# Half-width broadcasts doubled by ScalarE, and a reordered start and end, in a window-attention and mixture-of-experts kernel

## The chip, the cores and the metric

The kernel runs on 1 core of one Trainium2 chip. The metric is the device time of one execution in microseconds. Three runs of the kernel before gave 4324.14, 4325.08 and 4339.78: a median of 4325.08 us.

## What is computed

The input `x` is 2 images of 128 channels and 256 x 256 pixels in fp32. Two residual blocks follow each other:

```python
x = x + _L0_conv_ref(_ln_c(x), W_qkv, W_out, rel_height, rel_width)
t = tokens(x)                       # one token of 128 channels per pixel
t = t + _L0_ffn_ref(_ln_t(t), router_w, router_b, expert_w, expert_b)
```

`_ln_c` and `_ln_t` subtract the mean over the 128 channels and divide by the standard deviation. The first block is attention of 8 x 8 windows over 12 x 12 key windows, with 4 heads of 32 channels and relative position logits, masked so that each query pixel sees only keys of every second row and column. The second one routes each token: a softmax over 8 experts, the best two kept and scaled to sum to 1, and the sum of the two experts' 128 x 128 products weighted so.

## The kernel before

**Tiling.** Channels lie on the 128 partitions. The pixels are cut into 64 strips of 8 image rows (32 for each image), and each strip into 4 planes, the pixels of equal parity in rows and columns; the mask makes planes independent in the attention. A step of the main loop (L811) does the attention of plane `n` (256 in all) and a share of everything else, so that each engine has work at all times. Two image rows (512 tokens) are called a row here and written (strip, k), k from 0 to 3. The loop runs 7 steps past the last plane for what is left of the last rows.

**What a step holds.** For plane n: the scores (`scores`, L464, matmuls of L476 and L493), their exponential `pT` (L501), the weighted sums (`attend`, L505, matmuls of L514 and L524) and, on VectorE, the chain of sum transposed (L534), reciprocal, transposed back (L539) and output `o` (L544); then the output projection `po` (L552), added into `xt` (L557). For plane n+1: values, position products, keys and queries (`project`, L399: `pv` L349, `pu` L408, `pk` L422, `pq` L447), with ScalarE copying values, keys (`kcol`, L433 and L443) and queries (`qs`, L449) out of PSUM. The values go to DRAM (`send_values`, L368) and come back as key windows `vwin` (`take_values`, L380). For one finished row and one row that the attention will need: squares on ScalarE (L576), sums by matmul (`norms`, L565, L582), and their inverse deviations on VectorE and ScalarE (`rstd`, L222).

**The experts' way through the steps.** In the step after its norms a row is routed (`route`, L608: logits, their exponential on ScalarE at L620, ranks, gates), and gates, mean and rates are transposed and written to DRAM (`spread`, L650). They are read back as broadcasts, the same 512 numbers on every partition: the rates `rb` of the first norm (`fetch_rstd`, L664), the mean `sb` (`fetch_means`, L693) and the eight gates `gb` (`fetch`, L682). In each `fetch` an engine writes one column of the buffer first, so that the DMA's wait for the buffer is taken by that engine. A step later `means` adds the mean to the row (L701), `times` multiplies by each gate (L707, six on VectorE, experts 5 and 7 on GpSimd), and eight matmuls sum up in one bank of PSUM (`product`, L716), experts 0 to 3 at the end of that step, 4, 6, 7 and 5 in the next one. `end` (L722) adds them to the row, and `store` (L752) writes it out. GpSimd also applies the first norm (`ln1`, L273) to rows of coming strips.

**What sets the order.** Inside the main loop the order of every engine's instructions is the order of the program (`tc.manual_schedule`, L810). The helpers are generators, and the loop advances them piece by piece with `next`. Ahead of the loop a scheduler orders the instructions. Nearly all DMAs are issued from SP's queue, in order: one that waits for a landing holds up those behind it. L825 aligns TensorE's instruction stream at the start of each step from step 6 to the last plane: it fills up with NOPs until the next instruction has slot 157 in a block of 256.

**Start.** Ahead of the loop stand the loads of `x` and of the weights, the preparation of the weights (L157 to L196), the first norms of the rows of strip 0 and of two more (`first_norms`, L282, three stages each: squares, sums and a copy; statistics; spreading by transposes and `ln1`), and the projection of plane 0.

Of the kernel before, what the change touches and what calls it, by code (L numbers as in the profile page):

```python
# [17 lines left out]
P = 128  # L18
HEADS, DH = 4, 32
E = 8  # L20
# [26 lines left out]
BLOCK, FIRST_LIMIT = 256, 99  # L47
NU = 9


@with_exitstack
def kernel(
# [46 lines left out]
    nc.scalar.preload_act_table_set("natural_log_exp_and_others")  # L99

# [37 lines left out]
    for j in range(4):  # L138
# [17 lines left out]

    wmean = ctile([P, 3, 1], "wmean")  # L157
    nc.vector.tensor_reduce(wmean, wall[:, 0:3, :], AX.X, ALU.add)
    nc.vector.tensor_scalar_mul(wmean, wmean, 1.0 / C)
    nc.vector.tensor_tensor(  # L160
        wall[:, 0:3, :], wall[:, 0:3, :], wmean.broadcast_to([P, 3, P]), ALU.subtract
    )
    wt = ctile([P, 4, P], "wt")
    pw = mm_tile("pw")
    for j in range(4):
        nc.tensor.transpose(pw[:, j * P : (j + 1) * P], wall[:, j, :], ident)
    nc.vector.tensor_copy(wt.rearrange("p j c -> p (j c)"), pw)
    nc.vector.tensor_scalar_mul(wt[:, 0, :], wt[:, 0, :], SCALE)
    wq, wk, wv, wo = (wt[:, j, :] for j in range(4))

    relT = []
    for rname, rsb in zip(("relh", "relw"), relsb):
        pr = mm_tile(f"p_{rname}")
        nc.tensor.transpose(
            pr[:, :n_rel], rsb.rearrange("r h d -> r (h d)"), ident[:n_rel, :n_rel]
        )
        rT = ctile([P, n_rel], f"{rname}T")
        nc.vector.tensor_scalar_mul(rT, pr[:, :n_rel], SCALE)  # L180
        relT.append(rT)
    mid = n_rel // 2
    lo = mid - 2 * (PR - 1)
    relbd = ctile([P, P], "relbd")
    nc.gpsimd.memset(relbd, 0.0)
    for h in range(HEADS):
        hp = slice(h * DH, (h + 1) * DH)
        for j in range(2):
            c0 = h * DH + NU * j
            nc.vector.tensor_copy(  # L190
                relbd[hp, c0 : c0 + NU], relT[j][hp, lo : lo + 2 * NU - 1 : 2]
            )
    wrel = ctile([P, P], "wrel")
    pr = mm_tile("p_wrel")
    nc.tensor.matmul(pr[:, :P], lhsT=wall[:, 0, :], rhs=relbd, start=True, stop=True)
    nc.vector.tensor_copy(wrel, pr[:, :P])  # L196
# [368 lines left out]
    def norms(f, c, nm):  # L565
# [13 lines left out]
        plt = mm_tile(f"plt{nm}")  # L579
# [84 lines left out]
    def fetch_rstd(gd, nm):  # L664

        rb = gates.tile([P, NT * P], F32, tag="rb", name=f"rb{nm}", bufs=2)
        nc.sync.dma_start(rb, to_all(gd, E + 1))
        return rb

    def to_all(gd, j):  # L670

        return gd[j * NT : (j + 1) * NT].rearrange("r k -> (r k)").partition_broadcast(P)

    class Experts:
# [7 lines left out]
        def fetch(self, e, eng):  # L682
# [8 lines left out]
            nc.sync.dma_start(self.gb[e], to_all(self.gd, e))  # L691

        def fetch_means(self):  # L693

            self.sb = gates.tile([P, NT * P], F32, tag="sb", name="sb%d_%d" % self.at, bufs=1)
            nc.sync.dma_start(self.sb, to_all(self.gd, E))  # L696
# [28 lines left out]
    class NoExperts:  # L725
        def fetch(self, e, eng):
            pass

        def fetch_means(self):
            pass  # L730
# [15 lines left out]

    to_store = []
# [9 lines left out]


# [14 lines left out]
    for _ in range(3):  # L773
# [36 lines left out]
    with tc.manual_schedule(engines={ET.PE, ET.DVE, ET.Activation, ET.Pool, ET.SP}):  # L810
        for n in range(n_planes + 7):  # L811
# [12 lines left out]
            if 6 <= n < n_planes:  # L824
# [5 lines left out]
            if gated and gated[0]:  # L830
                rout = route(*gated[0], *gated[2])
            next(rout, None)
            nxt.fetch(5, nc.scalar)
            for _ in rout:
# [3 lines left out]
            nxt.fetch(7, nc.scalar)  # L838
            if gated:
# [10 lines left out]
            next(ahead, None)  # L850
            next(ahead, None)
            for e in (4, 6, 7, 5):
                ex.product(e)


            f = (i - 1, pl) if 0 < i <= len(strips) else None
            c = row_at(n)
            if f or c:
                norm = norms(f, c, f"_{n}")
# [104 lines left out]
```

## Time and profile before

| | |
|---|---|
| median of three runs | 4325.08 us |
| the profiled execution | 4331.68 us |
| its span, first to last instruction | 4329.9 us |
| TensorE busy, 94,273 matmuls | 4220.6 us (97%) |
| VectorE busy | 3790.8 us (88%) |
| ScalarE busy | 1320.4 us (30%) |
| GpSimd busy | 1087.9 us (25%) |
| granted TensorE clock, mean | 0.991 |
| DMA: moved | 1022.17 MB, mean 236 GB/s |
| gates `gb`: 2,048 loads of 256 KB, issue to landing | 5.7 us (median) |
| means `sb`: 256 loads of 256 KB | 4.5 us |
| rates `rb`: 249 loads of 256 KB | 3.5 us |

An instruction's row tells its start, its length, its engine and line, what it writes and reads, and in brackets how long the engine stood idle before it and what ended that. PE is TensorE, PEld its weight loads, DVE VectorE, ACT ScalarE, POOL GpSimd, SP the queue that issues DMAs. "issue" means that the engine waited for nothing that the profile shows.

### The profile page before, as it was taken

The page shows a single profiled execution, that of the slowest core. Times are in us where ns is not written, and L with a number is a line of the kernel's source. Part 1 is how long each engine was busy: PE and PEld are TensorE (multiplying, and loading weights), DVE is VectorE, ACT ScalarE, POOL GpSimd, SP SyncE. Part 2 cuts the span into 40 slices and gives each one's busy share as a digit, 9 for nine tenths or more (in the row PEclk, how much of TensorE's full clock was granted, in tenths as well). Part 3 has the DMA queues.
Part 4 walks back from the last instruction along what each step waited for, and adds up shares of the span by engine and source line. Part 5 has one row for each costly group of instructions (what it writes and reads, how often), then busy time and mean ns, then how long its engine had stood idle before and what let it go on. Part 6 is the DMA issues. An engine that isn't in the chain of part 4 may idle for free. (4 is left out here: it accounts for less than half of the span.)

```text
span 4329.9 us, 224393 instructions
## 1 busy us (share of the span) xinstructions
PE 4220.6 (97%) x94273; PEld 2464.3 (57%) x94273; DVE 3790.8 (88%) x11850; ACT 1320.4 (30%) x3774; POOL 1087.9 (25%) x1126
## 2 busy tenths in 40 slices
PE   7899999999999999999999999999999999999987
PEld 5455555555555555555555555555555555555553
DVE  5798898898888889988889889898888898888877
ACT  3223333332333333233332333333323232333321
POOL 1222222222222222222222222222222222222211
PEclk9999999999999999999999999999999999999999
DMA  4787878788787877878788787887878788787865
GB/s 112 212 245 241 248 236 246 241 244 248 235 239 240 247 236 248 248 235 251 240 247 241 243 247 238 247 248 239 247 233 246 233 250 244 239 246 239 245 190 190
DMA packets 824578, 1022.17 MB, mean 236 GB/s; under 512 B 137634, under 2 KB 409634, under 8 KB 823594
## 3 DMA queue, kind: packets, MB, share of 16 engines
q1 hardware_dynamic: 822864, 1007.52, 76.5%
q8 instruction: 769, 12.60, 1.3%
q14 instruction: 215, 1.76, 0.1%
q10 hardware_dynamic: 730, 0.29, 0.0%
HBM read 863.78 MB, written 143.75 MB: 233 GB/s over the span
## 5 line engine op out<-in xcount | busy, mean ns | idle before, releaser
L716 PE MATMUL acc<-xe,ew 128*128 128x512 f32 x4096 | 1918.4, 601 | 20.7 <-DVE gb L690 14.5
L716 PEld LDWEIGHTS acc<-xe,ew 128*128 128x128 f32 x4096 | 758.4, 190 | 940.3 <-issue 872.7
L707 DVE TENSOR_TENSOR xe<-xs,gb 128x512 f32<-128x512 f32 x1536 | 950.4, 685 | 11.2 <-PE acc L716 1.6
L711 POOL COPY last<-xe 128x1 f32<-128x1 f32 x256 | 47.6, 186 | 3120.0 <-DVE gb L690 3110.9
L707 POOL TENSOR_TENSOR xe<-xs,gb 128x512 f32<-128x512 f32 x512 | 652.1, 1275 | 1.5 <-PE att L524 1.0
L493 PE MATMUL att<-qs,kcol 32*60 32x32 f32 x32768 | 395.3, 223 | 16.7 <-issue 15.9
L493 PEld LDWEIGHTS att<-qs,kcol 32*60 32x60 f32 x32768 | 390.3, 127 | 21.1 <-issue 20.5
L275 POOL TENSOR_TENSOR xn<-xt,rb 128x512 f32<-128x512 f32 x249 | 374.0, 1502 | 93.5 <-DMA rb<-gd 92.7
L524 PEld LDWEIGHTS att<-pT,vwin 64*32 64x32 f32 x32768 | 349.7, 105 | 47.2 <-issue 9.3
L524 PE MATMUL att<-pT,vwin 64*32 64x32 f32 x32768 | 348.4, 200 | 6.5 <-issue 5.5
L501 ACT ACTIVATE pT<-att 128x1024 f32<-128x1024 f32 x256 | 262.2, 1024 | 296.3 <-PE att L493 296.3
L349 PE MATMUL pv<-wt,xn 128*128 128x128 f32 x2048 | 301.9, 291 | 0.9 <-issue 0.9
L412 DVE STREAM_TRANSPOSE uT<-pu 128x512 f32<-128x512 f32 x256 | 183.5, 717 | 132.1 <-PE pu L408 127.2
L576 ACT ACTIVATE sq<-xt 128x512 f32<-128x512 f32 x505 | 292.6, 630 | 0.0
L396 DVE STREAM_TRANSPOSE au<-auT 128x512 f32<-128x512 f32 x256 | 269.7, 1053 | 9.0
L552 PE MATMUL po<-o,wt 128*128 128x512 f32 x512 | 266.4, 602 | 10.2 <-DVE o L544 6.6
L408 PE MATMUL pu<-xn,wrel 128*128 128x512 f32 x512 | 267.5, 604 | 0.9 <-issue 0.9
L433 ACT COPY kcol<-pk 128x560 f32<-128x560 f32 (+2 forms) x344 | 183.4, 533 | 276.5 <-PE pk L422 273.7
L422 PE MATMUL pk<-xn,wt 128*128 128x512 f32 (+2 forms) x528 | 261.9, 580 | 0.0
L447 PE MATMUL pq<-xn,wt 128*128 128x512 f32 x512 | 261.7, 592 | 0.0
L349 PEld LDWEIGHTS pv<-wt,xn 128*128 128x128 f32 x2048 | 252.3, 194 | 11.7 <-issue 1.3
L476 PEld LDWEIGHTS att<-au,keys 32*64 32x64 f32 x8192 | 118.2, 133 | 230.2 <-PE po L552 183.8
(2437 smaller groups left out, 4853.9 us busy)
## 6 DMA issues: line engine op xcount, KB each, us to landing
gb<-gd SPq DMA_DIRECT2D x2048, 256.0 KB, 5.7
vwin<-vrows SPq DMA_DIRECT2D x512, 240.0 KB, 5.1
xt<-in_x_dram SPq DMA_DIRECT2D x256, 256.0 KB, 6.6
sb<-gd SPq DMA_DIRECT2D x256, 256.0 KB, 4.5
out_dram<-xt SPq DMA_DIRECT2D x256, 256.0 KB, 6.0
rb<-gd SPq DMA_DIRECT2D x249, 256.0 KB, 3.5
vrows<-vr SPq DMA_DIRECT2D x168, 256.0 KB, 3.9
vrows<-vr SPq DMA_DIRECT2D x160, 128.0 KB, 3.7
```

Source lines behind the costliest of these rows:

```text
L275: eng.tensor_tensor(xn[i % 2][:, :, :, k, 1 : PC + 1], ln1_src(i, k).rearrange("p (y j x) -> p y x j", y=2, x=2), rb.rearrange("p (y j x) ...
L349: nc.tensor.matmul(pv[:, j * P : (j + 1) * P], lhsT=xp[:, k, 1 : PC + 1], rhs=wv, start=True, stop=True,)
L396: nc.vector.transpose(au.rearrange("p m a s -> p a s m"), auT[n % 2])
L408: nc.tensor.matmul(pu, lhsT=wrel, rhs=inner, start=True, stop=True)
L422: nc.tensor.matmul(pk[:, : m * PC], lhsT=wk, rhs=xp[:, part[0] : part[0] + m, 1 : PC + 1], start=True, stop=True,)
L493: nc.tensor.matmul(sc[rows, h, 32 * t : 32 * t + 32], lhsT=kk[hp, half * HP + t, 0:NK], rhs=qs[hp, m0 : m0 + 2].rearrange("p m a s -> p (m ...
L501: nc.scalar.activation(pT, att[:, :, 0:HQ], AF.Exp)
L524: nc.tensor.matmul(av[hp, half, 32 * t : 32 * t + 32], lhsT=vv[rows, t, hp], rhs=pT[rows, h, 32 * t : 32 * t + 32], start=True, stop=True,)
L552: nc.tensor.matmul(po, lhsT=wo, rhs=state["o"].rearrange("p f z -> p (f z)"), start=True, stop=True)
L576: nc.scalar.activation(sq, src, AF.Square)
L707: eng.tensor_tensor(self.xe[e], self.xs, self.gb.pop(e), ALU.mult)
L716: nc.tensor.matmul(self.acc, lhsT=ew[:, e, :], rhs=self.xe.pop(e), start=(e == 0), stop=not self.xe)
```

## The change

Gates, means and rates are loaded to partitions 0 to 63 alone, and ScalarE copies them to the other 64 at places written out in the loop. At the start, the first stage of the first norms stands ahead of the preparation of the weights. In steps 0 to 5 (`FILL`) keys and queries of the next plane are projected after the norms' matmuls, whose sums go to the experts' bank of PSUM. TensorE's stream is aligned once at the top (with a branch over the filling), in steps 7 to 249 as before, and in step 6 and steps 250 to 255 after the experts' products instead. The 7 steps past the last plane are replaced by `finish_last`: row (62,3) and the four rows of the last strip. It does the norms and routing of those four rows in one batch, loads their gates on all partitions into free row buffers, and multiplies and sums row by row. The diff, cut; `wmean` to `wrel` is moved unchanged:

```diff
-BLOCK, FIRST_LIMIT = 256, 99
+BLOCK, FIRST_LIMIT, SUMS_AT = 256, 99, 40
+FILL = 6
...
+    nc.tensor.addr_align(BLOCK, offset=51, max_nops=0)
...
-    def norms(f, c, nm):
+    def norms(f, c, nm, plt=None):
...
-        plt = mm_tile(f"plt{nm}")
+        plt = plt or mm_tile(f"plt{nm}")
...
-        nc.sync.dma_start(rb, to_all(gd, E + 1))
+        fetch_half(rb, gd, E + 1)
...
+    def fetch_half(tile_, gd, j):
+        nc.sync.dma_start(tile_[0:SLOT], to_all(gd, j, SLOT))
+    def other_half(tile_):
+        nc.scalar.copy(tile_[SLOT:], tile_[0:SLOT])
...
-            nc.sync.dma_start(self.gb[e], to_all(self.gd, e))
+            fetch_half(self.gb[e], self.gd, e)
+        def double(self, e):
+            other_half(self.gb[e])
...
-            nc.sync.dma_start(self.sb, to_all(self.gd, E))
+            fetch_half(self.sb, self.gd, E)
+        def double_means(self):
+            other_half(self.sb)
...
+    def finish_last(ex, nxt, gated):
...
+        for _ in route(*f, *made):
+            pass
+        nxt.fetch(5, nc.scalar)
+        nxt.fetch(7, nc.scalar)
...
+        gd = spread(f, None, made[0], "_c")
+        fetch_all(0, gd)
+        for e in (4, 6, 7, 5):
+            ex.product(e)
+        plt = mm_tile("plt_l")
+        for r, at in enumerate(rows):
...
+            nc.scalar.activation(sq, src, AF.Square)
...
+        nxt.means()
+        ex.end()
+        for e in (0, 1, 2, 3, 4, 6, 5, 7):
+            nxt.double(e)
+            nxt.times(e, nc.gpsimd)
+        for e in (0, 1, 2, 3, 4, 6, 5, 7):
+            nxt.product(e)
...
+        nc.scalar.activation(r_, u, AF.Ln, scale=4.0)
...
+        for r in range(4):
...
+                nc.sync.dma_start(to[k], gT[:, r, k])
+            if r == 1:
+                fetch_all(1, gds[0])
+        store(*to_store.pop())
+        fetch_into(
+            2, gds[1], [gates.tile([P, CH], F32, tag="gb", name=f"gl2_{e}", bufs=8) for e in range(E)]
+        )
...
+        for row, at in enumerate(todo):
+            xes = multiply(at, row)
+            if row < 2:
+                fetch_all(row + 3, gds[row + 2])
...
+            products(accs[:, row % 4], xes)
...
-    for _ in range(3):
+    next(parts[0])
+    wmean = ctile([P, 3, 1], "wmean")
...
+    for part in parts[1:]:
+        next(part)
+    for _ in range(2):
...
-        for n in range(n_planes + 7):
+        for n in range(n_planes):
...
-            if 6 <= n < n_planes:
+            usual = n > 6 and row_at(n - 1) is not None
+            if usual:
                 nc.tensor.addr_align(BLOCK, offset=BLOCK - FIRST_LIMIT)
...
+            nxt.double(0)
+            nxt.double(1)
             next(rout, None)
             nxt.fetch(5, nc.scalar)
+            nxt.double(2)
...
             nxt.fetch(7, nc.scalar)
+            nxt.double(3)
...
-            next(ahead, None)
-            next(ahead, None)
+            filling = n < FILL
+            if not filling:
+                next(ahead, None)
+                next(ahead, None)
             for e in (4, 6, 7, 5):
                 ex.product(e)
+            if n >= 6 and not usual:
+                nc.tensor.addr_align(BLOCK, offset=SUMS_AT)
...
+            nxt.double(4)
+            nxt.double(6)
...
-                norm = norms(f, c, f"_{n}")
+                room = None
+                if filling:
+                    room = ps_acc.tile([P, 512], F32, tag="acc", name=f"plt_{n}")
+                norm = norms(f, c, f"_{n}", room)
             next(norm, None)
+            nxt.double(5)
+            nxt.double(7)
             next(attn, None)
             nxt.means()
             new.fetch_means()
+            if row:
+                other_half(row[2])
+            new.double_means()
...
             next(norm, None)
+            if filling:
+                next(ahead, None)
+                next(ahead, None)
...
+        finish_last(ex, nxt, gated)
```

## The prediction

> **What bounds the kernel now.** I read the busy times first, then the stages between chosen exponentials (`pT`, L501: one per step, 256 in all), then the order of time around each idle stretch of TensorE. The first view has, per stage, its length, each engine's busy time with its count, the granted clock, the DMA engines' share and GB/s.
>
> ```profile
> core 0: us, PE busy (x) PEld busy (x) DVE busy (x) ACT busy (x) POOL busy (x), PEclk, DMA share, GB/s
> 0.00:33.12 33.12, 20.82 (x341) 15.02 (x342) 16.63 (x53) 9.91 (x21) 6.87 (x35) 1.00 0.49 150
> 33.12:101.74 68.62, 55.14 (x1709) 35.72 (x1708) 34.69 (x97) 23.15 (x56) 6.86 (x6) 0.88 0.39 98
> 101.74:127.82 26.08, 10.40 (x353) 7.39 (x353) 11.89 (x47) 4.93 (x13) 1.49 (x1) 0.73 0.46 134
> 127.82:162.83 35.01, 31.12 (x729) 18.68 (x730) 27.89 (x87) 10.36 (x31) 8.76 (x9) 0.95 0.68 193
> 162.83:4108.43 3945.60, 3918.75 (x88329) 2289.85 (x88330) 3533.33 (x11039) 1232.61 (x3529) 1022.76 (x1027) 1.00 0.80 243
> 4108.43:4241.70 133.27, 117.05 (x2473) 68.61 (x2473) 104.50 (x325) 30.68 (x85) 22.73 (x27) 0.93 0.65 189
> 4241.70:4329.90 88.20, 67.34 (x346) 29.02 (x346) 61.92 (x206) 8.75 (x40) 18.44 (x21) 0.89 0.56 191
> ```
>
> The long stage holds 240 steps: 16.44 us each, TensorE 99% busy. An undisturbed step takes 16.24 us (every start in one lies that much after its like in the step before), so 240 x 16.24 = 3897.6, and 48 us are jitter, spread over 92 steps. TensorE is the bound and the change takes no matmul from it here; only those 48 us can be won. The other stages are where it idles: 13.5 us, 15.7, 16.2 and 20.9 in the second, third, sixth and seventh rows.
>
> ```profile
> 69.21 1.67 PE L552 MATMUL po<-o,wt 128*128 128x512 f32 x2 [2.19 <-DVE o L544]
> ...
> 124.89 1.16 PE L476 MATMUL att<-au,keys 32*64 32x128 f32 x32 [13.93 <-issue]
> ...
> 2468.73 2.31 PE L716 MATMUL acc<-xe,ew 128*128 128x512 f32 x5 [0.85 <-issue]
> ...
> 4180.47 0.70 PE L476 MATMUL att<-au,keys 32*64 32x128 f32 x32 [2.94 <-issue]
> ```
>
> These four, from TensorE's order of time, are the four kinds of idleness. In the first six steps the projection waits 2.2 us for VectorE's chain (L534 to L544). Ahead of step 6 and of steps 250 to 255 it waits for "issue": there stand the NOPs of L825, 201 before step 6 and 63 or 67 before each of the last, at 0.071 us each in the trace (201 x 0.071 = 14.3). The 31 NOPs of a usual step cost nothing: they run out while the product before them is computed. The third is jitter: no semaphore, TensorE's sequencer without instructions.
>
> **Part 1, broadcasts to 64 partitions and ScalarE's copies.** A step sends eight gates, the means and the rates: ten loads of 256 KB become 128 KB, 1.28 of 3.9 MB. The jitter goes with instruction blocks that come late: the trace has 3 fetches of 16 KB a step, and in the long steps the third mostly starts 14.5 to 16 us after the scores' start, else near 12.5; from 12 us to 3.5 us of the next step the 16 DMA engines are full. The bounds of the gain are 0 and 48 us.
>
> ```profile
> 325.38:326.38 1.00, 1.00 (x99) 0.96 (x83) 0.93 (x3) 0.00 (x0) 0.00 (x0) 1.00 0.98 361
> ...
> 335.68:336.58 0.90, 0.90 (x21) 0.55 (x14) 0.83 (x3) 0.00 (x0) 0.90 (x2) 1.00 0.83 236
> 336.58:337.48 0.90, 0.90 (x3) 0.38 (x2) 0.86 (x2) 0.00 (x0) 0.90 (x1) 1.00 1.16 236
> ```
>
> The columns are those of the first view. The first row is gates on 128 partitions: 361 GB/s. The two others are the loads of `vwin`, 60 partitions each: 236. A rule speaks against the change here: the Trainium skill, "SBUF — State Buffer", section "Door 1: The DMA port swizzle", says that partitions 0 to 63 reach only 8 of 16 ports, so that such a load has half the bandwidth. By the rule (8 x 27.2 = 218 GB/s) 128 KB take 0.60 us, by the row 0.56, 256 KB now 0.71 (256 KB/361): half the bytes save 0.11 to 0.15 us, not 0.35. But `vwin` comes in packets of 512 bytes, which are dearer, so the row is a lower end for packets of 2 KB; the upper is 361 and 0.36 us. Ten loads free 1.1 to 3.5 of 13 us of engine time a step. I take 28 of the 48 us, nearer to full relief, as only fetches over some 2 us late cost.
>
> ScalarE is in order and busy 5.0 of 16.24 us. A copy of 512 columns costs 0.63 us (as the squares, 1.15 for two overlapped); ten add 6.3: 11.3 of 16.24. What counts is where each waits.
>
> ```profile
> 2002.59 0.23 ACT L620 ACTIVATE lg<-lg 128x32 f32<-128x32 f32 x1 [2.02 <-DVE lg L619]
> ...
> 2003.82 1.02 ACT L501 ACTIVATE pT<-att 128x1024 f32<-128x1024 f32 x1 [0.92 <-PE att L493]
> ...
> 2006.62 0.64 ACT L433 COPY kcol<-pk 128x560 f32<-128x560 f32 x1 [1.04 <-PE pk L422]
> ```
>
> The scores begin at 2001.79. Copies 0 and 1 stand ahead of the routing's exponential, which runs at 0.80 after that; behind it VectorE waits (L629 on), and with it the gates' DMA and the SP queue. Over 143 undisturbed steps gates 0, 1, 2 land in the median at 0.49, 1.34, 2.07 of the next step, 3 at 3.45, 4 at 4.33. With today's landings copy 1 would end at 1.34 + 0.63 = 1.97, 1.2 us late. Ahead of gate 1 in its stretch lie four shortened loads (rates, means, gates 0 and 1), and the backlog of gates 5 and 7 before them: at 0.3 us each they bring it to about 0.1, at 0.11 to 0.9. At 0.1 the copies end by 0.75 and nothing waits. I take that. Copies 2 and 3 fall before and after the exponential of 2.03 and the values' copy, ending at 1.8 and 4.5, the keys' copy (4.83) is not hindered; 4 and 6 push the squares by 1.3 us to 8.7, needed at 10.74; the rates' half ends near 11, POOL uses it at 11.92. The wait price is zero while those hold; if not, see the rival.
>
> **Part 2, opening.** The first row-norm stage is put ahead of the weights' preparation. Its matmuls cannot start before the router weights land (11.67, idle ended by a DMA), so they gain nothing, while 12 VectorE operations (3.0 us by their rows: wt, relT, eight relbd, wrel) that lay ahead of that landing may now fall behind it. No DMA moves; POOL's one memset goes behind others and is needed no earlier. Bounds -1 and +3.5; I take +1.
>
> **Part 3, steps 0 to 5.** Keys' and queries' matmuls (1.24 + 0.95 us) go behind the norm's, into the 2.2 us wait for `o`. Their copies on ScalarE go behind too, and behind the copied rates, whose landing (about 8.5 us into the step) is then the next limit: copies end near 10.4, the next score matmuls with keys need them. `xt`'s marker follows, not urgent. So a step of 13.7 us becomes some 11.1. Part of that is the idle time, part the clock. The Trainium skill, "TensorE: Matmul & The Clock Gate", section "Why this matters for your kernels", allows gaps up to about 3 us before half clock; here gaps of 2.2 us go with a granted clock of 0.88. By the rule five intervals save 5 x 2.0 = 10 us, by the row up to 5 more: I take 13 (5 to 19).
>
> Step 6: the stream is aligned to slot 51 at the top and to slot 40 in step 6 after the projections. 4,849 sequencer instructions stand before that point in the trace: 51 + 4849 is 36 modulo 256, a few of them ahead of the alignment, so 5 to 10 NOPs instead of 201. It saves 14 us (13.93 idle), and 2 more in 127.82:162.83 for the matmuls at half clock (pv, pu 2.08 and 1.75 us against 1.16 and 1.02). A phase missed by one would leave up to 255 NOPs.
>
> **Part 4, steps 249 to 255.** Their 133.27 us are 19.6 above 7 x 16.24. The NOPs now stand after the four products, where TensorE has 3.6 us of products and 3 us of projections queued; 63 x 0.071 = 4.5 us are covered but for some 0.3; only step 250 has about 94 (6.7 us) and shows 2. Idle 16.2 plus cold matmuls some 5, less 2 + 5 x 0.3 + reserve: 17 saved (10 to 21).
>
> **Part 5, the last four rows.** Now five rows follow each other at 11 us: route, write gates (3.1 us landing), load, multiply. In the change, from the last exponential: row (62,3) routed at 16.1 as now; means and sum 17.4; four rows' norm matmuls 18.1 (4 x 0.65 after 15.5); eight copies on ScalarE hold its logarithm until 21.2; then VectorE's batch: large operations 1.2 us for 1,024 elements (0.425 at 256, 0.685 at 512: 1 ns each), three of them, the rest about 4.5: gates at 29.3. Row (62,2)'s eight products all go to POOL, 8 x 1.275 from 17, done at 27.5 behind that batch. Written and landed 33. Four rows load 36 x 256 KB at 0.67 = 24 us, done near 59. TensorE is later: five rows x 8 x 0.86 = 34.4 from 30.5, to 65. Sum and store 4.2 (4325.70 to the end): 69 instead of 88.2: 19 saved (5 to 25, the lower if row buffers come free late).
>
> **Sum.** The profiled execution took 4331.68 (span 4329.90, 1.78 around it). +1 - 13 - 14 - 2 - 28 - 17 - 19 = -92: 4240. It lay 6.6 above the median of the runs, 4325.08; jitter varies from run to run and shrinks with the change, so I carry over a third of that: 4238.
>
> **Rivals.** (a) The transfer is hidden anyway: half a tile at half the speed, jitter stays, and landings come just in time. For it: the rule and the 236 GB/s. Against: small packets. 4240 + 28 = 4268. (b) ScalarE sets the pace, the slower end: gate 1 lands near 0.9 to 1.0, copy 1 ends at 1.6, the routing's exponential is 0.8 late; gates, values, `vwin` and the next gates 0 and 1 all follow from it on SP, so the delay repeats each step: 240 x 0.79 = 190 on 4268 gives 4458. It decides from 64/240 = 0.27 us a step on. Against it: VectorE has 1.5 us free a step, and `o` is ready 1.0 us before its matmul. (c) Start and tail don't pay: row buffers wait, the filled steps starve for instructions; only NOPs and jitter go: 4332 - 28 - 17 - 14 + 2 = 4275.
>
> **Chances.** Forecast 0.56, (a) 0.17, (c) 0.13, (b) 0.10, all at full size 0.04 (4205). The range 4195 to 4295 holds the first, (a) and (c) with their spread and leaves out (b) and a little. 0.5% (22 us) is what a measurement can tell from no change: faster 0.85, within 0.05, slower 0.10 from (b) and its small forms.
>
> **What would show it.** Undisturbed steps still 16.24 us, L620 0.8 us after the scores' start, 240 steps under 3920 us, DMA share under 0.7; steps 0 to 4 near 11 us at full clock; no 14 us gap; last stage near 70 us. Wrong if L620 comes later and the steps stretch, if half loads take as long as whole ones, or if tail loads leave TensorE waiting.

## The result and the profile after

The changed kernel takes 4300.94 us (median of six runs, 4293.61 to 4308.35), the kernel before beside it 4324.61: a ratio of 0.9942, 95% interval 0.9924 to 0.9960. That is faster by 24 us: clear of no change by its interval, though hardly more than the 0.5% that the prediction gave a measurement. It is 63 us short of the forecast of 4238 and above the range of 4195 to 4295. The profiled execution took 4298.63, its span 4296.8, which is 33.1 less than before.

The first view is again the table by stage of the changed kernel, cut at the same exponentials (`pT`, now L462). Its columns are those of before.

```profile
core 0: us, PE busy (x) PEld busy (x) DVE busy (x) ACT busy (x) POOL busy (x), PEclk, DMA share, GB/s
0.00:31.30 31.30, 22.27 (x341) 15.32 (x342) 15.71 (x53) 9.90 (x22) 7.14 (x36) 0.95 0.52 159
31.30:93.46 62.16, 52.75 (x1709) 34.12 (x1709) 35.30 (x100) 25.29 (x61) 6.89 (x6) 0.95 0.35 100
93.46:108.61 15.15, 10.08 (x353) 6.72 (x353) 10.80 (x44) 7.82 (x18) 1.50 (x1) 1.00 0.55 151
108.61:142.27 33.66, 32.21 (x734) 19.65 (x735) 26.92 (x84) 22.57 (x50) 8.76 (x9) 0.95 0.54 147
142.27:4087.31 3945.04, 3935.75 (x88325) 2310.75 (x88324) 3522.12 (x11042) 2693.91 (x5929) 1023.13 (x1027) 1.00 0.62 163
4087.31:4203.71 116.40, 114.23 (x2473) 66.13 (x2473) 102.10 (x316) 69.03 (x151) 22.71 (x27) 0.97 0.48 139
4203.71:4296.80 93.09, 68.83 (x346) 28.49 (x345) 62.72 (x117) 13.09 (x30) 23.78 (x19) 0.87 0.52 168
```

Three things are to be seen. Step 6 and the steps from 249 on (rows three and six) gained 10.9 and 16.9 us. The 240 steps of row five took 3945.04, as before (3945.60), though the DMA engines fell from 0.80 to 0.62 busy: what the loads freed did not arrive. And the tail, the last row, is 4.9 us longer, where 19 were to be saved.

TensorE's order of time, at the four places shown of before:

```profile
65.09 1.12 PE L513 MATMUL po<-o,wt 128*128 128x512 f32 x2 [1.18 <-ACT kcol L404]
...
103.63 0.69 PE L437 MATMUL att<-au,keys 32*64 32x128 f32 x32
...
4128.37 0.67 PE L475 MATMUL att<-pT,ones 64*32 64x256 f32 x16 [1.80 <-issue]
...
4210.22 0.67 PE L475 MATMUL att<-pT,ones 64*32 64x256 f32 x16 [3.06 <-issue]
```

The projection of a filled step no longer waits for `o` but for the keys' copy, 1.18 us. Step 6's scores begin with no wait, where 13.93 us of NOPs stood. The NOPs of step 250 cost 1.80, those of step 255, which has no projection behind which they could run out, 3.06. The group rows of TensorE's two bursts of small matmuls in the 240 steps show what became of the jitter (busy us, mean ns, then idle us and what ended it); first the kernel before, then the changed one.

```profile
L493 PE MATMUL att<-qs,kcol 32*60 32x32 f32 x30720 | 368.2, 222 | 16.2 <-issue 15.4
L524 PE MATMUL att<-pT,vwin 64*32 64x32 f32 x30720 | 326.6, 200 | 6.1 <-issue 5.1
```

```profile
L454 PE MATMUL att<-qs,kcol 32*60 32x32 f32 x30720 | 378.4, 222 | 0.0
L485 PE MATMUL att<-pT,vwin 64*32 64x32 f32 x30720 | 335.6, 200 | 0.0
```

The idle time of 16.2 and 6.1 us is gone: no late instructions any more. But the same 2 x 30,720 matmuls are busy for 378.4 and 335.6 us instead of 368.2 and 326.6. The gain of 22.3 is eaten by 19.2 of longer bursts, and idle elsewhere. In most steps of before each start lay 16.24 us after its like; now the median is 16.38. So the theories to be told apart were: (A) the relief is worth what was forecast and ScalarE's copies eat it; (B) the form of the loads, 64 partitions at a time, stretches TensorE's bursts. The expectations below letter their theories each in its own way.

### The profile page after: what moved, and what is told of

The parts are those of the page before. It is cut to its first block, busy times and chain, and to the rows that moved or that the text cites. A ratio compares the mean times of both kernels' runs of the same rounds, so it can differ in the third digit from the quotient of the medians.

```text
span 4296.8 us, 226188 instructions
## 1 busy us (share of the span) xinstructions
PE 4236.1 (99%) x94273; PEld 2481.2 (58%) x94273; DVE 3775.7 (88%) x11752; ACT 2841.6 (66%) x6258; POOL 1093.9 (25%) x1125
## 5 line engine op out<-in xcount | busy, mean ns | idle before, releaser
L693 PE MATMUL acc<-xe,ew 128*128 128x512 f32 x4016 | 1877.6, 600 | 2.5 <-POOL xe L684 0.7
L641 ACT COPY gb<-gb 64x512 f32<-64x512 f32 x2008 | 1181.2, 616 | 237.8 <-DMA gb<-gd 205.0
L693 PEld LDWEIGHTS acc<-xe,ew 128*128 128x128 f32 x4016 | 741.7, 190 | 900.1 <-issue 853.7
L684 DVE TENSOR_TENSOR xe<-xs,gb 128x512 f32<-128x512 f32 x1500 | 927.6, 685 | 8.6
L454 PE MATMUL att<-qs,kcol 32*60 32x32 f32 x32768 | 404.5, 222 | 4.6 <-issue 4.6
L454 PEld LDWEIGHTS att<-qs,kcol 32*60 32x60 f32 x32768 | 402.7, 126 | 5.3 <-issue 5.0
L485 PEld LDWEIGHTS att<-pT,vwin 64*32 64x32 f32 x32768 | 361.9, 105 | 45.7 <-issue 6.0
L485 PE MATMUL att<-pT,vwin 64*32 64x32 f32 x32768 | 360.6, 200 | 5.5 <-issue 5.4
L641 ACT COPY rb<-rb 64x512 f32<-64x512 f32 x249 | 153.8, 618 | 229.9 <-DMA rb<-gd 229.0
L462 ACT ACTIVATE pT<-att 128x1024 f32<-128x1024 f32 x256 | 262.0, 1023 | 64.0 <-PE att L454 59.8
```

The lines of the kernel that those rows point to most:

```text
L454: nc.tensor.matmul(sc[rows, h, 32 * t : 32 * t + 32], lhsT=kk[hp, half * HP + t, 0:NK], rhs=qs[hp, m0 : m0 + 2].rearrange("p m a s -> p (m ...
L485: nc.tensor.matmul(av[hp, half, 32 * t : 32 * t + 32], lhsT=vv[rows, t, hp], rhs=pT[rows, h, 32 * t : 32 * t + 32], start=True, stop=True,)
L641: nc.scalar.copy(tile_[SLOT:], tile_[0:SLOT])
L684: eng.tensor_tensor(self.xe[e], self.xs, self.gb.pop(e), ALU.mult)
L693: nc.tensor.matmul(self.acc, lhsT=ew[:, e, :], rhs=self.xe.pop(e), start=(e == 0), stop=not self.xe)
```

## The experiments

Each ratio is to runs of the kernel before on the same chip. Stage times are from one profiled execution each; a tail is counted from the last exponential on.

**Part 1 undone.** Whole loads, no copies; parts 2 to 5 kept.

```diff
-        nc.sync.dma_start(tile_[0:SLOT], to_all(gd, j, SLOT))
+        nc.sync.dma_start(tile_, to_all(gd, j))
...
-        nc.scalar.copy(tile_[SLOT:], tile_[0:SLOT])
+        pass
```

> The changed kernel with part 1 undone: all ten broadcasts to 128 partitions, no copies by ScalarE; opening, pads and tail as changed. Theory A (relief and copies cancel: lighter DMA traffic takes away the late instruction blocks, some 40 us, and ScalarE's copies slow TensorE's bursts of small matmuls by as much): total like the changed kernel, 4301 +-6; the 240 steps 3945, with single long stalls back. Theory B (neither does anything): also 4301, so this run alone tells only what part 1 is worth. Theory C (part 1 is what gains): slower than 4315.

Measured: 4287.29, ratio 0.9920 (0.9904 to 0.9936). The interval overlaps that of the changed kernel, so part 1 brings nothing that can be measured; by the medians it rather costs some 10 us. None of the theories named for this run had it below 4295. The 240 steps took 3937.48, with the bursts as before (366.2 and 324.8 us busy, 11.2 and 4.3 idle).

**Copies without relief.** Whole loads, and the copies kept (only the first of the two edits).

> The changed kernel with broadcasts to all 128 partitions and ScalarE's ten copies kept (they write what is there already): the price of the copies without the relief. Theory A: 240 steps near 3985 to 3995, total about 4345. Theory B: 4301. If copies 0 and 1 wait for gates that land as late as before (0.5 and 1.3 us into the step), steps stretch by up to 0.8 us: total up to 4490.

Measured: 4394.38, ratio 1.0160 (1.0136 to 1.0184), the 240 steps 4033.84: the copies cost 96 us in these steps when gates land as late as before. The waits in them (us in total, times, longest) show rival (b) at work:

```profile
ACT gb L641 <- DMA gb<-gd: 387.4, 327, 4.0
...
DVE cmp L590 <- ACT lg L581: 200.5, 203, 3.3
...
PEld pq L408 <- ACT vr L318: 114.6, 145, 2.4
```

ScalarE stands 387 us before copies whose gate has not landed; behind it the routing's exponential holds VectorE up in 203 of 240 steps, and the values' copy holds up the queries' matmuls. In the changed kernel the same three rows are

```profile
ACT gb L641 <- DMA gb<-gd: 202.2, 213, 2.6
...
DVE cmp L590 <- ACT lg L581: 78.9, 117, 1.8
...
PEld pq L408 <- ACT vr L318: 17.9, 34, 1.4
```

so the earlier landings keep rival (b) small, but not at nothing, as "nothing waits" had it.

**Half loads without copies.** The other single part: eleven fixed buffers, zeroed once, take the half loads; the copies go.

```diff
-        nc.scalar.copy(tile_[SLOT:], tile_[0:SLOT])
+        pass
...
-            self.gb[e] = gates.tile([P, NT * P], F32, tag="gb", name=f"gb{nm}", bufs=8)
+            self.gb[e] = kept["gb"][next(turn_gb) % 8]
```

> Left out: the copies of gates, means and rates to the upper 64 partitions; the loads stay half as wide and go into eleven fixed buffers that are zeroed once at the start (some 7 us of GpSimd there), so the upper halves of the gated inputs are zero. It prices the relief alone, where the run of the two parts together left 240 steps at 3945 us and the run with neither of them at 3937. Theory A (relief is worth what the prediction gave it and the copies on ScalarE ate it): the stretch from step 8 to step 248 falls to about 240 x 16.24 = 3898, at most 3910, and the time to about 4255. Theory B (the narrower loads are what spreads small delays over the steps, the copies cost nothing): the stretch stays at 3935 to 3945, the score bursts' median near 1347 ns, the time 4290 to 4300. If relief does nothing at all the bursts are at 1285 ns and the late weights come back as in the kernel before (waits of over 0.3 us in some 90 steps), with 3937 to 3945.

Measured: 4299.22, ratio 0.9948 (0.9932 to 0.9964; the shared buffers lengthen the tail to 107.4, so the stage counts): 3931.79 for the 240 steps. Theory A falls: without a single copy the steps are only 13.3 us shorter, not 35 to 47.

```profile
L454 PE MATMUL att<-qs,kcol 32*60 32x32 f32 x30720 | 380.1, 222 | 0.0
L485 PE MATMUL att<-pT,vwin 64*32 64x32 f32 x30720 | 332.9, 200 | 0.0
```

TensorE never waits here (0.4 us in 240 steps), and its bursts are as long as in the changed kernel.

**Half the columns instead of half the partitions.** As many bytes saved, all 128 partitions written; the same fixed buffers, no copies.

```diff
-        nc.sync.dma_start(tile_[0:SLOT], to_all(gd, j, SLOT))
+        half = gd[j * NT : j * NT + NT // 2].rearrange("r k -> (r k)").partition_broadcast(P)
+        nc.sync.dma_start(tile_[:, 0 : NT // 2 * P], half)
...
```

> Left out: the second half of the columns of gates, means and rates, and the copies; each load takes 256 of 512 columns to all 128 partitions, into the same fixed zeroed buffers as in the run of half loads without copies. As many bytes are saved as there, but the writes are spread over all partitions. Theory B1 (loads that write only 64 partitions hold up TensorE's operand reads): the score bursts' median is back at 1285 to 1290 ns, the steps' median at 16.24 to 16.28, and steps 8 to 248 take 3900 to 3912 us, as the late weights stay away too. Theory B2 (the bursts are stretched by anything that the shorter loads change, such as the time at which transfers run): the bursts stay at 1335 to 1350 ns and the stretch at 3925 to 3940. If packets of 1 KB take as long as those of 2 KB there is no relief: waits for instructions come back, 3935 to 3945 with bursts at 1285.

Measured: 4269.84, ratio 0.9876 (0.9856 to 0.9897), the 240 steps 3899.01: 16.24 us a step from the 5th percentile to the 95th.

```profile
L454 PE MATMUL att<-qs,kcol 32*60 32x32 f32 x30720 | 359.9, 222 | 0.0
L485 PE MATMUL att<-pT,vwin 64*32 64x32 f32 x30720 | 321.1, 200 | 0.0
```

This is B1, with the stage 1 us below its range. Against the run with 64 partitions the two bursts are 32.0 us shorter, and the stage 32.8: nearly the whole difference lies in these two rows. The saved bytes are worth 46.6 us against the kernel before, of its 48 us of jitter, but jitter differs from one execution to the next: against the two kernels with whole loads and the changed start and end (3937.48 above, 3932.18 in the last part) they are worth 38.5 and 33.2. So the relief is 33 to 47 us, and loads of 64 partitions give 32.8 of it back.

**Which property of a half load?** Two more forms, again without copies: the halves in turn (even gates to partitions 0 to 63, odd ones to 64 to 127), and 64 rows on every second partition.

```diff
-        nc.sync.dma_start(tile_[0:SLOT], to_all(gd, j, SLOT))
+        lo = j % 2 * SLOT
+        nc.sync.dma_start(tile_[lo : lo + SLOT], to_all(gd, j, SLOT))
...
```

> Left out as in the run of half loads without copies, but the loads go in turn to the lower and to the upper 64 partitions (even gates and the means to the lower, odd gates and the rates to the upper), so that loads that overlap write different halves. Theory B1 with its density (what counts is how many bytes are written to one partition in a time): the bursts fall from 1339 ns to between 1295 and 1320, and the stretch from 3932 to 3905-3922 us. If a load to half the partitions is by itself what holds TensorE up, or B2: 1330 to 1350 and 3927 to 3940.

```diff
-        nc.sync.dma_start(tile_[0:SLOT], to_all(gd, j, SLOT))
+        nc.sync.dma_start(tile_[0:P:2], to_all(gd, j, SLOT))
...
```

> Left out as in the run of half loads without copies, but each load of 64 rows of 2 KB goes to partitions 0, 2, 4 to 126 instead of 0 to 63: as many partitions and bytes, spread over the whole height. Theory G (what stretches the bursts is that 64 neighbouring partitions lie behind half of the ports): score and attention bursts take 360 and 321 us in 240 steps and steps 8 to 248 take 3898 to 3906. Theory H (bytes per partition: 64 partitions as such): 375 to 380 and 330 to 335 us, and 3927 to 3935.

Measured: in turn 4295.73 (0.9933, 0.9917 to 0.9950), 3930.91 in the 240 steps, bursts 377.3 and 334.8; every second 4291.88 (0.9944, 0.9925 to 0.9964), 3926.00, bursts 372.6 and 335.1.

```profile
L454 PE MATMUL att<-qs,kcol 32*60 32x32 f32 x30720 | 372.6, 222 | 0.0
L485 PE MATMUL att<-pT,vwin 64*32 64x32 f32 x30720 | 335.1, 200 | 0.0
```

Spreading over the height frees the queues further (DMA share 0.63 to 0.55) but shortens the stage by 5.8 of 32.8 us only, about what the two kernels with whole loads differ by (5.3), and alternating does nothing: theory G explains the smaller part at most. What stays is that all loads of 64 rows stretch the bursts and all loads of 128 rows don't.

Two other causes can be set aside from the traces' single records. It isn't the data rate: between the first and the last start of a score burst (128 matmuls) the transfers moved 360 GB/s in the run of whole loads and 146 in that of half columns, both with a median of 1286 ns from start to start, and 142 to 195 in the three runs of half loads without copies, with 1328 to 1339. Nor is it the late instruction blocks in a milder form. Those stop TensorE at two places of the program, ahead of the 18th matmul of a score burst and of the 108th of an attention burst. At these two the kernel before has a delay of over 60 ns in 52 and 47 of 240 steps, part 1 undone in 40 and 32, half loads without copies in none (the two other forms in none and 3). Half loads delay the score bursts mostly from 0.3 to 0.5 us into the burst on, and the attention bursts at no fixed matmul.

In the attention bursts one thing goes with the delay: the loads of the key windows, in packets of 512 bytes to 60 partitions. In the three runs of half loads without copies, 130 bursts ran while these held 12 or more of the 16 DMA engines for over 0.3 us, and 119 of them were over 40 ns longer than the usual 1145 ns from first to last start; of the 403 in which they never did, 42 were. In the two runs of half columns (here and below) none of 11 such bursts was longer. So it seems to take both; by what path they stretch a burst is open.

**The copies by themselves.** Half columns, with the ten copies put back.

> The run of half columns, with ScalarE's ten copies a step of 64x512 put back where the changed kernel has them (what they copy is left half empty, as there: the second half of the columns is missing). It prices the copies without the stretched bursts. If the copies cost by themselves what the difference of two runs showed, steps 8 to 248 go from 3899 to 3908 to 3916 us, with waits of VectorE for the routing's exponential behind copy 1. If they only cost in company with stretched bursts: 3899 to 3903. If loads of 128 partitions land later than halves do, gates 0 and 1 hold ScalarE up as in the run of whole loads with copies, and the stretch is above 3930.

Measured: 4271.01, ratio 0.9899 (0.9882 to 0.9915), the 240 steps 3900.17: the copies cost 1.2 us. ScalarE waits here for gates 135 times, 74.9 us in all (213 times and 202.2 in the changed kernel), VectorE for the routing's exponential 8.9 us (16 times; 78.9 in the changed kernel), and TensorE for the values' copy 2 us in all. With half loads the copies cost 13.3 (3945.04 less 3931.79; six profiled kernels with the changed part 1 lay at 3940 to 3952, so 8 to 20). ScalarE's 6.3 us a step are thus nearly free where gates land early, and not where they land late. Whether the 13 us come from the landings or from the stretched bursts beside them, these runs don't tell.

**The fill of the first six steps off.** `FILL = 0`.

> The changed kernel with the fill of the first six steps switched off: their keys' and queries' matmuls go back ahead of the products. Theory F (the reordering is worth what the stage shows): steps 0 to 5 go from 62.2 to 67 to 69 us as in the kernel before, the waits of 1.2 us for the keys' copy ahead of the projection become waits of 2.2 us for VectorE, and nothing else moves by over 2 us. Rival (the 6.5 us that the stage won came from something else, the freed transfers or the clock): 63 to 65 us.

Measured: 4305.69, ratio 0.9962 (0.9947 to 0.9978), steps 0 to 5 66.81 us. TensorE's waits for VectorE in these steps are those of before again (us in total, times, longest):

```profile
PE po L513 <- DVE o L505: 8.8, 4, 2.3
PE po L513 <- DVE m__4_1568 L193: 2.4, 1, 2.4
```

The kind of wait is as theory F has it. The size is not settled: fourteen profiled kernels with the fill took 59.2 to 67.6 us in this stage (median 62.8), the two without 66.8 and 68.6. The difference of the medians is 5, with one kernel's spread as large.

**The tail.** First the old one put back (the last rows step by step, all else as changed).

> The changed kernel with the seven steps past the last plane as before in place of the batched tail (their loads are half-width with copies). From the last exponential on the changed kernel takes 93.1 us, before 88.2. If the NOPs in step 255 (3.1 us and half clock after it, about 5 us) are the whole difference, this run is like the changed one: 4301 +-3, 93 us. If the batch itself costs, it is faster by what it costs: 4296, 88 us or less.

Measured: 4296.55, ratio 0.9943 (0.9929 to 0.9957); the tail takes 87.17 us against 93.09. Part 5 costs 5.9 by this pair. A single tail is not known that well: the run with the fill off has the changed kernel's tail, and there it took 89.92. Three edits of the new tail follow, one at a time. Each of these three kernels ran once (4301.46, 4296.93 and 4296.13 us), so what counts is the tail and its rows. The first keeps the gate chain's values in PSUM:

```diff
-        nc.vector.tensor_tensor(u, r_, r_, ALU.mult)
+        nc.vector.tensor_tensor(u, r_, p4[:, :, E], ALU.mult)
+        room = mm_tile("room_l")
+        var, u = u, room[:, 0:m]
...
-        lg = small.tile(by_e, F32, tag="lg_l", name="lg_l", bufs=1)
+        lg = room[:, m : m + m * E].rearrange("p (q e) -> p q e", e=E)
...
```

> The changed kernel, with the intermediate values of the last four rows' gate chain (variance and logits) kept in PSUM, so that each VectorE step has one PSUM operand. Theory C (VectorE steps that touch only SBUF are held while GpSimd multiplies; those with a PSUM operand are not): the seven steps of 0.7 to 1.2 us fall to 0.2 to 0.3, the gates' transpose comes 5 to 6 us earlier (T0 + 32.5 instead of 38.0 after the start of step 255), and the tail falls from 93.1 to 87 or 88. Rival (the steps are long for their own dependence on each other, or the rows are bound elsewhere): the durations stay, or they fall and the rows begin earlier but the end moves by under 2 us because the gates' loads are late then.

VectorE's and GpSimd's order of time in the changed kernel:

```profile
4227.22 0.90 DVE L829 TENSOR_TENSOR u_l<-r_l 128x16 f32<-128x16 f32 x1
4228.16 0.17 DVE L830 SCALAR_TENSOR_TENSOR u_l<-u_l,plg_l 128x16 f32<-128x16 f32 x1
...
4231.82 1.19 DVE L836 SCALAR_TENSOR_TENSOR rs_l<-u_l,r_l 128x16 f32<-128x16 f32 x1
...
4233.37 0.98 DVE L843 TENSOR_TENSOR lg_l<-lg_l,rb 128x128 f32<-128x128 f32 x1
4234.38 0.28 DVE L844 TENSOR_REDUCE mx_l<-lg_l 128x16 f32<-128x128 f32 x1
...
4236.00 1.22 DVE L855 TENSOR_TENSOR cmp_l<-lg_l 128x1024 f32<-128x1024 f32 x1
...
4239.77 0.29 DVE L861 SCALAR_TENSOR_TENSOR rank_l<-rank_l,lg_l 128x128 f32<-128x128 f32 x1
...
4225.60 9.87 POOL L684 TENSOR_TENSOR xe<-xs,gb 128x512 f32<-128x512 f32 x8 [12.83 <-PE plt_l L805]
```

and with the values in PSUM:

```profile
4233.43 0.17 DVE L829 TENSOR_TENSOR u_l<-r_l,plg_l 128x16 f32<-128x16 f32 x1
...
4235.45 0.17 DVE L838 SCALAR_TENSOR_TENSOR rs_l<-room_l,r_l 128x16 f32<-128x16 f32 x1
...
4235.99 0.30 DVE L846 TENSOR_TENSOR room_l<-room_l,rb 128x128 f32<-128x128 f32 x1
...
4237.30 1.77 DVE L859 TENSOR_TENSOR cmp_l<-lg_l 128x1024 f32<-128x1024 f32 x1
4239.10 2.17 DVE L862 TENSOR_TENSOR cmp_l<-cmp_l,ties 128x1024 f32<-128x1024 f32 x1
...
4242.56 1.21 DVE L865 SCALAR_TENSOR_TENSOR rank_l<-rank_l,lg_l 128x128 f32<-128x128 f32 x1
...
4231.82 11.79 POOL L684 TENSOR_TENSOR xe<-xs,gb 128x512 f32<-128x512 f32 x8 [12.54 <-DMA gb<-gd]
```

The same steps take 0.17 to 0.30 us instead of 0.90 to 1.19, while GpSimd multiplies. Theory C holds, and the ranks' step (L861, L865 here) is its control: unchanged, with both inputs in SBUF, it takes 0.29 us after GpSimd's end (4235.47) in the changed kernel and 1.21 before it (4243.61) here. The comparisons, which stayed in SBUF too, also fall within GpSimd's time now: 1.77 and 2.17 where they took 1.22. The gates' transpose starts 34.7 us after the tail's start instead of 37.5, and the tail takes 89.49: 3.6 less, of the expected 5 to 6.

Then step 255 without NOPs:

```diff
-            if n >= 6 and not usual:
+            if n >= 6 and not usual and n < n_planes - 1:
```

> The changed kernel without the filling instructions of step 255 alone, where there is no projection left for TensorE to do while its sequencer runs them. Theory D (step 255 pays for them in full): its attention begins some 3 us earlier, its bursts keep the full clock, and the tail falls from 93.1 by 4 to 5, to 88 or 89. Rival (the fetch of the following code is what they buy, and without them it is late by as much): the tail stays within 1.5 us of 93.1, with a wait for instructions inside the attention's burst.

```profile
4210.26 0.66 PE L475 MATMUL att<-pT,ones 64*32 64x256 f32 x16
...
4214.24 0.42 PE L543 MATMUL plt<-sq,rw 128*32 128x128 f32 x7 [1.61 <-issue]
```

The tail takes 88.26, 4.8 less (1.7 less than the 89.92): the attention follows the products with no gap. The rival has its share, a wait of 1.61 us for instructions a little later.

Last, a PSUM tile for each row's products:

```diff
-        accs = ps_att.tile([P, 4, CH], F32, tag="att", name="accs")
+        accs = [mm_tile(f"accs{row}") for row in range(5)]
...
```

> The changed kernel, with a PSUM tile of its own for each of the last five rows' products instead of one tile of four banks. Theory E (a row's products wait for the addition of the row before because they share a tile): the wait of about 1.5 us ahead of each row goes, the rows follow each other at 7.13 us where their gates are there, and the tail falls from 93.1 by 4 to 6. Rival (the gates' landing sets the rows): under 2 us.

The five rows' products in the changed kernel, and with a tile for each row:

```profile
4243.09 10.12 PE L789 MATMUL accs<-xel,ew 128*128 128x512 f32 x16 [6.44 <-DVE xel L782]
4257.35 9.82 PE L789 MATMUL accs<-xel,ew 128*128 128x512 f32 x16 [4.14 <-DVE xt L901]
4268.66 7.13 PE L789 MATMUL accs<-xel,ew 128*128 128x512 f32 x16 [1.49 <-DVE xt L901]
4277.28 7.13 PE L789 MATMUL accs<-xel,ew 128*128 128x512 f32 x16 [1.49 <-DVE xt L901]
4285.80 7.13 PE L789 MATMUL accs<-xel,ew 128*128 128x512 f32 x16 [1.39 <-DVE xt L901]
```

```profile
4250.07 16.46 PE L789 MATMUL accs<-xel,ew 128*128 128x512 f32 x32 [6.44 <-DVE xel L782]
4267.51 1.98 PE L789 MATMUL accs<-xel,ew 128*128 128x512 f32 x4 [0.98 <-DVE xel L782]
4270.00 6.28 PE L789 MATMUL accs<-xel,ew 128*128 128x512 f32 x14 [0.50 <-DVE xel L782]
4276.53 1.12 PE L789 MATMUL accs<-xel,ew 128*128 128x512 f32 x2 [0.26 <-DVE xel L782]
4278.20 12.28 PE L789 MATMUL accs<-xel,ew 128*128 128x512 f32 x28 [0.55 <-DVE xel L782]
```

The waits of 1.4 to 4.1 us for `xt`, the addition of the row before (L901), are gone; the five rows take 40.4 us (4250.07 to 4290.48) instead of 49.8, and the tail 82.77: 10.3 less, twice what was expected, because the second row had waited 4.14 us and not 1.5, and the first two rows also run faster (16.46 us for both, where they took 10.12 and 9.82).

**What the runs point to.** Part 1 undone and the tail's three edits together:

> Whole-width loads without copies (part 1 undone), parts 2 to 5 kept, and the three repairs of the tail together: no filling instructions in step 255, the gate chain's values in PSUM, a PSUM tile per row of products. If the repairs add up (4.8 + 3.6 + 10.3 us in their single runs) the tail goes from 91.6 to 73 to 75 us and the time from 4287 to about 4269, range 4262 to 4276. If they overlap, above all since loads of 36 x 256 KB take 24 us at the least, the tail ends at 78 to 82 and the time at 4274 to 4279.

Measured: 4284.31 (4273.61 to 4285.54), ratio 0.9897 (0.9880 to 0.9915). The tail is at 76.39, 15.2 less than with part 1 undone alone, of 18.7 in the single runs. This beats both kernels; against part 1 undone alone (0.9920) the intervals overlap. Last, the relief by another way: gates rounded to bf16, and so half as many bytes on all 128 partitions.

```diff
-            self.gb[e] = gates.tile([P, NT * P], F32, tag="gb", name=f"gb{nm}", bufs=8)
+            self.gb[e] = gates.tile([P, NT * P], BF16, tag="gb", name=f"gb{nm}", bufs=8)
...
+            gh = small.tile([P, 32], BF16, tag="gh", name=f"gh{nm}")
+            nc.vector.tensor_copy(gh, gT[:, 0])
```

> Whole-width loads, no copies, the repaired tail as before, and the eight gates of a step rounded to bf16 and kept so in DRAM and SBUF (the last four rows' and all means and rates stay fp32); so only the gates' rounding differs from the reference. Each gate's load is 128 KB to 128 partitions. It is the relief of part 1 by another way. If theory B1 is the whole story (it is the bytes that free the queues, and the 64 partitions that stretch the bursts), the bursts' median is 1285 to 1290 ns, steps 8 to 248 take 3900 to 3910 us against 3932 to 3937 with fp32 loads, and the time is 4284 - 33 = about 4250. If VectorE or GpSimd are slower with a bf16 operand, or the rounding's step on VectorE (0.2 us ahead of the gates' store) delays what waits for the gates, a new wait of the products for the multiplications shows, and the stretch is 3930 or more.

Measured: 4238.02 (4230.40 to 4242.87), ratio 0.9814 (0.9798 to 0.9830). The row of its 240 steps, in the table's columns:

```profile
146.94:4047.80 3900.86, 3899.35 (x88329) 2282.59 (x88329) 3569.76 (x11277) 1234.22 (x3529) 968.00 (x1027) 1.00 0.62 180
```

3900.86, with bursts of 360.9 and 321.1 us, and with all gates in place: the short bursts of half columns don't come from what was left out there. So the jitter can be won, at the price of the gates' rounding. That the time is the one forecast for the change is chance: whole-height loads, rounded gates and a repaired tail are not in it.

## Why the prediction failed

| step | forecast, us | measured, us |
|---|---|---|
| start | +1 | -1.8 |
| steps 0 to 5 | -13 | -6.5 |
| step 6 | -14 | -10.9 |
| steps 6 to 8 | -2 | -1.3 |
| the 240 steps | -28 | -0.6 |
| steps 248 to 255 | -17 | -16.9 |
| tail | -19 | +4.9 |
| sum | -92 | -33.1 |

(Measured: the stages of the two profiled executions, one taken from the other.) Of the 59 us that are missing, 27 lie in the 240 steps and 24 in the tail.

**The 240 steps: the step that failed.** "I take 28 of the 48 us, nearer to full relief" was right about the bytes: late instruction blocks are all but gone in every run with half the bytes (at the two places above, 99 delays in 240 steps before, 1 in the changed kernel), and 33 to 47 us can be had. The amount that loads would free, 1.1 to 3.5 us of DMA time a step, holds as well: 0.80 of 16.44 us became 0.62 of 16.44, 3.0 us. That is far from the low end, which the rule of half the bandwidth gave: packets of 2 KB took 117 ns in the mean of the changed kernel's 240 steps, 101 before. (256 KB at 361 GB/s are 0.73 us, not 0.71, so each saving was set 0.02 too low.) What failed is that a half load was costed by its length alone. As first bound "0 and 48" stood in the text, but the only reason for the low end was that half a load might take as long as a whole one; that it makes TensorE's own work longer had no term. It costs 32.8 us. Then the price of the copies, "zero while those hold": they did not hold. Copy 1 begins in the median step 0.40 us after the scores' start, held by its own gate in half of the steps and by copy 0 in the others, and ends at 1.02, where 0.75 was taken; the routing's exponential follows at 1.10, not at 0.80. VectorE waits 78.9 us for it in all, and the copies together cost 13.3 us. So -46.6 + 32.8 + 13.3 = -0.5: three differences of stage times in a row, each with the spread of single executions (5 us for whole loads, 12 with the changed part 1). Rival (a), 4268, has the right sign for these steps, but its reason is wrong: the transfer was not hidden anyway. Rival (b) is what happens when the relief is missing (96 us where the text had 190: the exponential came at 1.80 in the median step, 1.0 us late, but only 0.40 us a step reached the time).

**The tail: the other step that failed.** The new tail was to end at 69 us and ended at 93.1. The rows' matmuls were to begin at 30.5 and began at 39.4; they were to take 34.4 and took 49.8. The first 8.9 are the NOPs of step 255, which part 4's "covered" did not cover there (4.8 by their own run), and a chain on VectorE "about 4.5" beside "eight products" on POOL, costed as if the two engines did not touch (3.6 by its own run). The Trainium skill, "SBUF — State Buffer", section "Who interferes with whom", says that a VectorE instruction with two SBUF inputs contends with a GpSimd instruction that reads SBUF; the rows above agree, 0.90 to 1.19 us against 0.17 to 0.30 with one input in PSUM. It should have been weighed in the prediction. Of the rows' 15.4 us, 9.4 are a tile of PSUM that all rows share: `accs` was read as four banks, and costed as if only the bank that is rewritten had to be free. The other 6.0 stay with a tile for each row (40.4 us): a row takes 7.13 us at the least, where 6.88 was set, the first two run slower (16.46), and some 2.3 us are waits for multiplied inputs.

**Steps 0 to 5.** Right in kind: the wait for `o` went. What is late next was named, the copies behind the rates' landing, but their end was given to the next scores. It is this step's projection that waits for them (1.2 us; 2.50 in step 6, which with a stall of 2.57 for instructions is more than the 3.1 missing there). Stalls of 1.8 and 2.1 us for instructions, in steps 0 and 3, had no term. Measured half of the forecast, within its 5 to 19, on a stage that differs by up to 8 us between kernels with the fill.

**What held, and what was luck.** That TensorE's NOPs cost next to nothing behind the products held in steps 251 to 254 (15.6 to 15.8 us each). That steps 248 to 255 came out to 0.1 us is chance, for three terms cancel. Step 250, foreseen as the exception, took 21.2 us (17.8 to 22.3 in all kernels), 5 above a usual step: behind its wait of 1.80 us the granted clock was 0.50 from 4131 to 4133. The four steps behind it took half a microsecond less each than the 16.24 that was set. And step 255's wait of 3.06 us, counted here at 0.3, falls behind the last exponential and so into the tail. The start's +1 became -1.8, 0.8 beyond its lower bound, on a stage with a spread of some 3 us. Rival (c), 4275, was right that the tail doesn't pay, though its rows waited for the tile of the row before and not for row buffers; the filled steps did starve for instructions, but half of their gain came. Together with (a) it gives 4275 + 28 = 4303 against 4300.94. That is chance too: the reasons were others, and both together had no number.

## What to carry to other kernels

A load that is made smaller can also be made to write fewer partitions, and that is a different change: here halving the bytes in the way that keeps all partitions was the better one. Look for the price in the busy time of the engine that bounds, not in its waits alone. When work is moved to an in-order engine ahead of a chain, its price depends on when its inputs land: the same copies cost 1, 13 and 96 us here. In a batch on VectorE beside GpSimd, keep one operand in PSUM, and give each independent accumulation a PSUM tile of its own.

## What was not expected of the hardware

Loads of 64 rows of 2 KB made TensorE's bursts of small matmuls 4 to 6% longer (380.1 and 332.9 us of 240 steps against 359.9 and 321.1), without any wait that the profile would show; loads of 128 rows at about twice the data rate (360 against 142 to 195 GB/s) didn't. The Trainium skill, "SBUF — State Buffer", section "Who interferes with whom", says that DMA never contends with a compute engine. These runs show that it is not without effect on one: here the measurement decides, with the path open. VectorE's steps on 16 values a partition took 0.9 to 1.2 us beside GpSimd's multiplications, and GpSimd's own eight took 9.87 us there and 11.79 beside the comparisons.
